# A linear-attention and patch-FFT block pair in one kernel: the normaliser made ahead of its spread, the first contraction behind the inverse transform, and k's first bias from its scaled weight

## The chip, the cores and the metric

The kernel runs on one core of one Trainium2 chip. A time is the time of one execution on the device in microseconds (us); the figure for the kernel before is the median of three runs, 3594.4 us (3587.12 to 3594.8). The profile is of one further execution, which took 3585.28 us.

## What is computed

The input x holds eight images of 384 channels and 64 x 64 pixels, in 32-bit floats. Two blocks follow each other, each with a group norm in front and the input added behind:

```python
def reference(x, ...):
    x = x + attention(_gn(x))       # layer 0
    x = x + patch_filter(_gn(x))    # layer 1
    return x

def _gn(v, G=32, eps=1e-5):         # mean and variance of 12 channels x 64 x 64
    g = v.reshape(B_, G, C_ // G, H_, W_)
    return ((g - mean(g)) / sqrt(var(g) + eps)).reshape(v.shape)

def attention(x):
    q = apply_rope_2d(conv1x1(x, Wq, bq))
    k = apply_rope_2d(conv1x1(x, Wk, bk))
    v = conv1x1(x, Wv, bv)
    q = elu(to_heads(q) * scale) + 1.0            # 6 heads of 64
    k = elu(to_heads(k)) + 1.0
    kv = einsum('bhnd,bhne->bhde', k, v)
    k_sum = k.sum(axis=2)
    normalizer = einsum('bhnd,bhd->bhn', q, k_sum)[..., None]
    out = einsum('bhnd,bhde->bhne', q, kv) / (normalizer + 1e-06)
    return conv1x1(out, Wfc, bfc)

def patch_filter(x):
    t = einsum('bchw,oc->bohw', x, w_in)
    tf = rfft2(patches_of_8x8(t)) * fft_filter
    t = irfft2(tf)
    t = depthwise_conv_3x3(t, w_dw)
    x1, x2 = t[:, :192], t[:, 192:]
    return einsum('bchw,oc->bohw', gelu(x1) * x2, w_out)
```

## The kernel before

**Tiles.** An image is 4096 tokens, cut into eight bands of 512 (8 rows of 64 pixels). The 384 channels lie as three tiles of 128 partitions. A band of x is one tile of 128 x 3 x 512. Every matmul writes a tile of the pool psum, which has eight buffers, all taken in turn under one tag; most larger intermediates share nine buffers of the pool work under the tag "w".

**Stages of an image.** First, while the image before is in its layer 1, its keys: per band and quarter of a band (128 tokens) pk (L421) projects x to k, px (L387) turns the same tokens of x, and later acc (L437) adds k by x into three sums. Instead of normalising x, the kernel scales the weight's rows (scale_weight) and adds a bias (k_bias, q_bias, v_bias). k_bias takes the group sums of wk, which sum_weight (L337) made once at image 0, with a matmul of one row of 32 groups.

Second, the queries of the image (queries, L801). q_project (L510) makes one band: nine matmuls pq in three thirds, on VectorE and ScalarE the bias and the rotation (L531, L545, L546, L547), then elu + 1 in three operations (L333, L334, L335), the last of which, L335 on VectorE, completes the band. q_normalise (L551) needs such a whole band and the sums of k: 12 matmuls pn (24 records in the trace), then on VectorE and ScalarE L564 to L572 make from them 1 / (normaliser + 1e-6), split into three bf16 parts. q_spread (L575) spreads these parts over the channels with 12 matmuls prb and multiplies them into q. project_out (L593) makes pf = mt x q, nine matmuls, and adds it to x (L601); mt is the product of k's sums, wv and wfc, made once per image by kv_finish (L446) in four steps, the last of them pm (L499) with nine copies. The loop runs over the bands: pq of band j + 2, then spread of j, then pn of j + 1, then pf of j - 1. At j = 2 output() contracts the last band of the image before; from j = 2 on the norm chain of the next image's layer 0 is advanced one step at a time (layer0_chain, L744).

Third, the norm of layer 1 (norm_chain, L260): four small groups of matmuls on PE, ps_m, ps_mc, ps_v, ps_r, with small VectorE operations and one square root (L299, with the load of ScalarE's table) between them. The main loop (L899) puts one quarter of the next image's keys behind each of them, then two more quarters, the chain's end, and the rest of the keys of band 1. The group that names a wait on hf is the normalised band, three ScalarE operations (L328), for the first matmuls of layer 1.

Fourth, layer 1 over the bands: pi (w_in), pd (forward transform), tf (times the filter, L635), pb (inverse transform, L644) into one of two ring buffers, the first tap (L691), and one band behind, the other eight taps on VectorE (L705, 24 operations of 512 columns per band), the gate (L711 to L714) and contract (L720): pw with w_out, addition to x (L735), the store of the band. At j = 2 and j = 3 contract(j - 2) stands between the forward and the inverse transform of band j; from j = 4 on behind the keys. Between these steps run the next image's keys, and stream_stats reads x of the image after it for its norm.

**Order.** The kernel is written for the Tile framework, which places the waits; PE's instructions stand in the order of the program, which is what the order of the calls of queries and of the main loop settles. VectorE's and ScalarE's instructions are ordered by the framework's scheduler. Loads and stores are issued from SP. The last image has no keys of a next image and runs its layer 1 in a loop of its own (L955).

Of the kernel before, what the change touches and what calls it, by code (L numbers as in the profile page):

```python
# [14 lines left out]
P = 128  # L15
C = 384
CT = 3
H = W = 64
N = H * W
NBAND = 8  # L20
# [3 lines left out]
NG = 32  # L24
# [92 lines left out]
def conv_blocks_kernel(ctx: ExitStack, tc: tile.TileContext, a: dict, out: bass.AP, nb: int):  # L117
# [142 lines left out]
    def norm_chain(b, layer, params):  # L260
# [52 lines left out]
        if layer == 0:  # L313
            shift = group_tile("shift")
            nc.vector.scalar_tensor_tensor(shift, gm, -1.0, rsg, ALU.mult, ALU.mult)
            params.append(shift)
# [33 lines left out]
    def k_bias(b, params):  # L350

        p_ = ps_tile(f"pbk_{b}")
        nc.tensor.matmul(p_[:, :C], params[2].to_broadcast([NG, P]), group_w["wk"], start=True, stop=True)
        t = small.tile([P, C], F32, tag="kbias", name=f"kbias_{b}", bufs=1)
        nc.vector.tensor_add(t, p_[:, :C], bk_bc)
        return t
# [236 lines left out]
    def project_out(b, j, q, mt):  # L593
        for m in range(CT):
# [6 lines left out]
            nc.vector.scalar_tensor_tensor(xm, p_, bfc[:, m : m + 1], xm, ALU.add, ALU.add)  # L601
        if j == 1:
            differences[b] = taps_pool.tile([P, CT, BT], F32, tag="dw", name=f"differences_{b}")
# [140 lines left out]
    def layer0_chain(b, prepared):  # L744
# [5 lines left out]
        for i, _ in enumerate(norm_chain(b, 0, params)):  # L750
            if b == 0 and i == 3:
                sum_weight(wk, "wk")
            yield
        scale_weight(wk, params)
        yield
        prepared += params, wk, k_bias(b, params)
# [44 lines left out]
    def queries(b, keys, gate, output):  # L801
# [12 lines left out]
        ahead = q_normalise(b, 0, q[0])  # L814
        for j in range(NBAND):
            rn = ahead
            if j < NBAND - 2:
                run(q_project(b, j + 2, wq, qbias, q))
# [5 lines left out]
            q_spread(b, j, q[j], rn)  # L824
            if j == 0:
                gate()
            if j < NBAND - 1:
                ahead = q_normalise(b, j + 1, q[j + 1])
            if j >= 1:
                project_out(b, j - 1, q.pop(j - 1), mt)  # L830
# [8 lines left out]
        project_out(b, NBAND - 1, q.pop(NBAND - 1), mt)  # L839
# [59 lines left out]
    for b in range(nb):  # L899
# [3 lines left out]
        chain, first, second = norm_chain(b, 1, params), keys.project(0), keys.project(1)  # L903
        for _ in range(4):
            next(chain)
            next(first, None)
        for _ in range(2):
            next(second, None)
        run(chain)
        run(second)  # L910
        if b == nb - 1:
            break
        for j in range(NBAND + 1):
            project = keys.project(j - 1 if j > 2 else NBAND)
            fill = chain_of(project, keys.accumulate(j if j < 2 else j - 2 if 3 < j < NBAND else NBAND))
            if j < NBAND:
                tf = []
                layer1 = expand_filter(b, j, normalised(b, j, params, (8, 8), "f"), tf)
# [4 lines left out]
                if j in (2, 3):  # L923
# [6 lines left out]
                first_taps(b, j)  # L930
            else:
# [22 lines left out]
    h = normalised(b, 0, params, (8, 8), "f")  # L954
# [58 lines left out]
```

## Time and profile before

| what | value |
|---|---|
| median of three runs | 3594.4 us (3587.12 to 3594.8) |
| the profiled execution, time on the device | 3585.28 us |
| its span, first to last instruction | 3583.5 us |
| mean clock granted to TensorE | 0.987 |
| VectorE, largest group: L705, the taps | 1055.4 us in 1520 operations |
| TensorE, largest group: L421, pk | 542.2 us in 1536 matmuls |
| ScalarE, largest group: L388, px copied out | 121.9 us in 256 operations |
| one image, start of its queries to start of the next one's | 439.5 us |
| mean traffic of the DMA queues | 81 GB/s |

Engines are named PE (TensorE's matmuls), PEld (its weight loads), DVE (VectorE), ACT (ScalarE), POOL (GpSimd) and SP (the queue that issues loads and stores). In a line of a timeline the first number is the start in us from the span's start, the second the length from the first instruction of the group to the end of its last; then engine, line of the kernel, operation, output <- inputs by the program's names, partitions x elements, and the number of records. A bracket at the end tells how long the engine had been idle and for what. In a table by windows there stand for each window its length, then busy time of the engines PE, PEld, DVE, ACT, POOL with the number of instructions that began there, the clock granted to PE, the share of the DMA engines' time, and GB/s. A list of waits names engine, the waiting operation, and the operation whose end ended the wait, then the sum, the number and the longest.

### The profile page before, as it was taken

The page shows a single profiled execution, that of the slowest core. Times are in us where ns is not written, and L with a number is a line of the kernel's source. Part 1 is how long each engine was busy: PE and PEld are TensorE (multiplying, and loading weights), DVE is VectorE, ACT ScalarE, POOL GpSimd, SP SyncE. Part 2 cuts the span into 40 slices and gives each one's busy share as a digit, 9 for nine tenths or more (in the row PEclk, how much of TensorE's full clock was granted, in tenths as well). Part 3 has the DMA queues.
Part 4 walks back from the last instruction along what each step waited for, and adds up shares of the span by engine and source line. Part 5 has one row for each costly group of instructions (what it writes and reads, how often), then busy time and mean ns, then how long its engine had stood idle before and what let it go on. Part 6 is the DMA issues. An engine that isn't in the chain of part 4 may idle for free.

```text
span 3583.5 us, 38458 instructions
## 1 busy us (share of the span) xinstructions
PE 3450.4 (96%) x14384; PEld 1881.5 (53%) x14384; DVE 2887.9 (81%) x4499; ACT 1810.7 (51%) x3242; POOL 123.0 (3%) x305
## 2 busy tenths in 40 slices
PE   7999999999999999999999999999999999999898
PEld 4544565455554555545564455644555445554454
DVE  6576898868987689885998759987699866997688
ACT  4445563456544565445653455534555354544453
POOL 0000000000000000000000000000000000000011
PEclk9999999999999999999999999999999999999999
DMA  6311223212322122321223212222123211222013
GB/s 212 105 61 50 80 89 120 74 51 71 106 105 75 47 78 99 114 78 45 97 71 126 66 45 97 92 105 66 45 97 113 95 54 36 71 78 80 21 42 91
DMA packets 124608, 290.76 MB, mean 81 GB/s; under 512 B 26069, under 2 KB 36486, under 8 KB 116230
## 3 DMA queue, kind: packets, MB, share of 16 engines
q1 hardware_dynamic: 123078, 282.39, 22.9%
q0 software_dynamic: 1008, 5.51, 0.8%
q8 instruction: 113, 1.85, 0.2%
q14 instruction: 73, 0.60, 0.1%
q10 hardware_dynamic: 336, 0.41, 0.0%
HBM read 232.44 MB, written 50.33 MB: 79 GB/s over the span
## 4 chain that ended last, share of the span: by engine, by line
PE 74%; DVE 20%; ACT 3%; issue 2%; DMA 0%; POOL 0%; SPq 0%; ACTq 0%; POOLq 0%
PE pf L597 13%; PE acc L437 12%; PE pk L421 12%; PE pq L517 12%; DVE dw L705 10%; PE pi L613 8%; PE pw L729 7%; PE pb L644 3%; PE px L387 2%; PE pd L627 2%; PE pn L556 1%; DVE qc L335 1%; DVE x L735 1%; DVE kc L424 1%; ACT ring L651 1%
## 5 line engine op out<-in xcount | busy, mean ns | idle before, releaser
L705 DVE SCALAR_TENSOR_TENSOR dw<-ring,w_dw,dw 128x512 f32<-128x512 f32 x1520 | 1055.4, 746 | 110.4 <-ACT dw L691 90.3
L421 PE MATMUL pk<-wk,x 128*128 128x384 f32 x1536 | 542.2, 490 | 0.1
L597 PE MATMUL pf<-qc,mt 128*128 128x512 f32 x1152 | 527.6, 614 | 0.0
L437 PE MATMUL acc<-xk,kc 128*128 128x385 f32 x1536 | 515.9, 488 | 10.8 <-DVE kc L335 10.8
L613 PE MATMUL pi<-w_in,hf 128*128 128x384 f32 x1536 | 510.2, 489 | 10.3 <-ACT hf L328 10.3
L517 PE MATMUL pq<-x,wq 128*128 128x512 f32 x1152 | 511.6, 596 | 0.7
L437 PEld LDWEIGHTS acc<-xk,kc 128*128 128x128 f32 x1536 | 287.5, 190 | 228.8 <-issue 46.0
L613 PEld LDWEIGHTS pi<-w_in,hf 128*128 128x128 f32 x1536 | 290.7, 191 | 209.9 <-ACT hf L328 12.1
L729 PE MATMUL pw<-gated,w_out 128*128 128x512 f32 x768 | 355.6, 612 | 15.0 <-DVE gated L714 14.5
L421 PEld LDWEIGHTS pk<-wk,x 128*128 128x128 f32 x1536 | 276.0, 190 | 170.4 <-issue 16.5
L597 PEld LDWEIGHTS pf<-qc,mt 128*128 128x128 f32 x1152 | 221.2, 196 | 271.9 <-issue 258.9
L517 PEld LDWEIGHTS pq<-x,wq 128*128 128x128 f32 x1152 | 214.9, 190 | 262.4 <-issue 243.0
L388 ACT COPY xk<-px 128x384 f32<-128x384 f32 x256 | 121.9, 477 | 388.1 <-PE px L387 388.1
L620 ACT COPY ht<-pi 128x384 f32<-128x384 f32 x256 | 121.8, 476 | 249.8 <-PE pi L613 237.4
L601 DVE SCALAR_TENSOR_TENSOR x<-pf,bfc,x 128x512 f32<-128x512 f32 x192 | 142.0, 740 | 125.7 <-PE pf L597 125.7
L729 PEld LDWEIGHTS pw<-gated,w_out 128*128 128x128 f32 x768 | 143.8, 195 | 187.1 <-issue 131.8
L545 ACT ACTIVATE qs<-pq,qbias 64x512 f32<-64x512 f32 x128 | 87.4, 683 | 298.0 <-DVE qc L531 264.3
L424 DVE TENSOR_TENSOR kc<-pk,kbias 128x384 f32<-128x384 f32 x256 | 140.9, 551 | 76.9 <-PE pk L421 75.6
L644 PEld LDWEIGHTS pb<-idft,tf 128*128 128x128 f32 x1536 | 180.6, 193 | 29.7 <-DVE tf L635 18.0
L644 PE MATMUL pb<-idft,tf 128*128 128x128 f32 x1536 | 185.4, 277 | 11.0 <-DVE tf L635 11.0
L651 ACT COPY ring<-pb 128x512 f32<-128x512 f32 x192 | 109.2, 581 | 163.4 <-PE pb L644 162.0
L333 ACT ACTIVATE qs<-qc 128x1536 f32<-128x1536 f32 x64 | 95.0, 1484 | 168.3 <-DVE qc L547 158.3
(149 smaller groups left out, 4006.7 us busy)
## 6 DMA issues: line engine op xcount, KB each, us to landing
tq<-in_tq SPq DMA_DIRECT2D x64, 1024.0 KB, 4.6
x<-in_x SPq DMA_DIRECT2D x64, 768.0 KB, 4.5
tk<-in_tk SPq DMA_DIRECT2D x64, 768.0 KB, 4.2
out_dram<-x SPq DMA_DIRECT2D x63, 768.0 KB, 3.3
xs<-in_x SPq DMA_DIRECT2D x56, 768.0 KB, 4.6
x<-y POOLq DMA_DIRECT2D x7, 768.0 KB, 5.7
wk<-in_wk SPq DMA_DIRECT2D x8, 576.0 KB, 4.0
wv<-in_wv SPq DMA_DIRECT2D x8, 576.0 KB, 6.0
```

The source lines that it names most:

```text
L388: nc.scalar.copy(xk[:, i, :C], px[:, :C])
L421: nc.tensor.matmul(pk[:, :C], tokens(t), wks[:, t, :], start=(t == 0), stop=(t == CT - 1))
L424: nc.vector.tensor_add(kc[:, i, :], pk[:, :C], bias)
L437: nc.tensor.matmul(acc[m][:, : C + 1], kf[:, i, m * P : (m + 1) * P], xk[:, i, :], start=(j == 0 and i == 0), stop=(j == NBAND - 1 and i = ...
L517: nc.tensor.matmul(p_, wqs[:, t, m * P : (m + 1) * P], xt[b, j][:, t, :], start=(t == 0), stop=(t == CT - 1),)
L597: nc.tensor.matmul(p_, mt[:, t, m * P : (m + 1) * P], q[:, t, :], start=(t == 0), stop=(t == CT - 1))
L601: nc.vector.scalar_tensor_tensor(xm, p_, bfc[:, m : m + 1], xm, ALU.add, ALU.add)
L613: nc.tensor.matmul(p_[:, :C], h[:, t, i * P : (i + 1) * P], w_in[:, t, :], start=(t == 0), stop=(t == CT - 1),)
L644: nc.tensor.matmul(patches[:, k // 2, k % 2], tf[:, k, m * P : (m + 1) * P], idft.rearrange("p (u n) -> p u n", u=2), start=True, stop=True,)
L651: nc.scalar.copy(t[:, m, 1:9, 1 : W + 1].rearrange("p r (b c) -> p r b c", c=8), p_.rearrange("p (b r c) -> p r b c", b=8, r=8),)
L705: nc.vector.scalar_tensor_tensor(acc[:, m], src, wd, acc[:, m], ALU.mult, ALU.add)
L729: nc.tensor.matmul(p_, w_out[:, s, m * P : (m + 1) * P], g[:, s, :], start=(s == 0), stop=(s == 1))
```

## The change

Four things are changed.

1. In queries, q_normalise of band j + 1 is called within q_project of band j + 2: behind its first third (behind its second for j = 0). Before, it was called behind the spread of band j. For band 7 (j = 6, where no further q is projected) it is called behind the first third of project_out of band 5, for which project_out becomes a generator that yields behind m = 0.
2. In the norm chain of layer 1 two quarters of the next image's keys, not one, are run behind the first step; after that one quarter behind each of the next three. normalised for band 0 is called straight behind the chain, before the keys that are left, and its tile is kept in ahead; the loop over the bands and the last image's loop take it from there.
3. contract(b, 0), which stood between the forward and the inverse transform of band 2, is called behind the inverse transform and the first tap of band 2, together with load_x(b + 1, 2). contract(b, 1) at j = 3 stays.
4. For image 0 k_bias no longer uses the group sums of wk: three matmuls of minus the mean (by channel) with the already scaled wk give it. The sum of wk by groups, which the images from 1 on use, is made in layer0_chain for image 1.

```diff
@@ -313,7 +313,7 @@
         if layer == 0:
             shift = group_tile("shift")
             nc.vector.scalar_tensor_tensor(shift, gm, -1.0, rsg, ALU.mult, ALU.mult)
-            params.append(shift)
+            params += shift, minus_mean
 
     def normalised(b, j, params, order, name):
 
@@ -347,10 +347,20 @@
         for i in range(CT):
             nc.vector.tensor_scalar(w[:, i, :], w[:, i, :], params[0][:, i : i + 1], factor, ALU.mult, ALU.mult)
 
-    def k_bias(b, params):
+    def k_bias(b, params, wk):
 
         p_ = ps_tile(f"pbk_{b}")
-        nc.tensor.matmul(p_[:, :C], params[2].to_broadcast([NG, P]), group_w["wk"], start=True, stop=True)
+        if "wk" in group_w:
+            nc.tensor.matmul(p_[:, :C], params[2].to_broadcast([NG, P]), group_w["wk"], start=True, stop=True)
+        else:
+            for t in range(CT):
+                nc.tensor.matmul(
+                    p_[:, :C],
+                    params[3][:, t : t + 1].to_broadcast([P, P]),
+                    wk[:, t, :],
+                    start=(t == 0),
+                    stop=(t == CT - 1),
+                )
         t = small.tile([P, C], F32, tag="kbias", name=f"kbias_{b}", bufs=1)
         nc.vector.tensor_add(t, p_[:, :C], bk_bc)
         return t
@@ -599,6 +609,8 @@
                 )
             xm = xt[b, j][:, m, :]
             nc.vector.scalar_tensor_tensor(xm, p_, bfc[:, m : m + 1], xm, ALU.add, ALU.add)
+            if m == 0:
+                yield
         if j == 1:
             differences[b] = taps_pool.tile([P, CT, BT], F32, tag="dw", name=f"differences_{b}")
         band_sums(b, 1, j, xt[b, j], differences.get(b))
@@ -747,13 +759,13 @@
             return
         wk = load_weight(b, "wk", k_runs) if b else first_wk
         params = []
-        for i, _ in enumerate(norm_chain(b, 0, params)):
-            if b == 0 and i == 3:
-                sum_weight(wk, "wk")
+        if b == 1:
+            sum_weight(wk, "wk")
+        for _ in norm_chain(b, 0, params):
             yield
         scale_weight(wk, params)
         yield
-        prepared += params, wk, k_bias(b, params)
+        prepared += params, wk, k_bias(b, params, wk)
 
     def chain_of(*chains):
         for c in chains:
@@ -811,23 +823,29 @@
         next(finish)
         prepared = []
         chain = layer0_chain(b + 1, prepared)
-        ahead = q_normalise(b, 0, q[0])
+        normaliser = {0: q_normalise(b, 0, q[0])}
         for j in range(NBAND):
-            rn = ahead
+
             if j < NBAND - 2:
-                run(q_project(b, j + 2, wq, qbias, q))
+                project = q_project(b, j + 2, wq, qbias, q)
+                for _ in range(2 if j == 0 else 1):
+                    next(project)
+                normaliser[j + 1] = q_normalise(b, j + 1, q[j + 1])
+                run(project)
             if j == 0:
                 run(finish)
                 mt = done[0]
             if 2 <= j < NBAND - 2:
                 next(chain, None)
-            q_spread(b, j, q[j], rn)
+            q_spread(b, j, q[j], normaliser.pop(j))
             if j == 0:
                 gate()
-            if j < NBAND - 1:
-                ahead = q_normalise(b, j + 1, q[j + 1])
             if j >= 1:
-                project_out(b, j - 1, q.pop(j - 1), mt)
+                output_ = project_out(b, j - 1, q.pop(j - 1), mt)
+                if j == NBAND - 2:
+                    next(output_)
+                    normaliser[j + 1] = q_normalise(b, j + 1, q[j + 1])
+                run(output_)
                 if j < NBAND - 2:
                     next(chain, None)
             if j == 2:
@@ -836,7 +854,7 @@
                 load_x(b + 1, j - 4)
             if j == NBAND - 2:
                 run(chain)
-        project_out(b, NBAND - 1, q.pop(NBAND - 1), mt)
+        run(project_out(b, NBAND - 1, q.pop(NBAND - 1), mt))
         return prepared
 
     for j in range(NBAND):
@@ -900,14 +918,14 @@
         prepared = queries(b, keys, gate, output)
         keys = Keys(b + 1, prepared)
         params = []
-        chain, first, second = norm_chain(b, 1, params), keys.project(0), keys.project(1)
-        for _ in range(4):
+        chain, more = norm_chain(b, 1, params), chain_of(keys.project(0), keys.project(1))
+        for quarters in (2, 1, 1, 1):
             next(chain)
-            next(first, None)
-        for _ in range(2):
-            next(second, None)
+            for _ in range(quarters):
+                next(more, None)
         run(chain)
-        run(second)
+        ahead = normalised(b, 0, params, (8, 8), "f")
+        run(more)
         if b == nb - 1:
             break
         for j in range(NBAND + 1):
@@ -915,12 +933,13 @@
             fill = chain_of(project, keys.accumulate(j if j < 2 else j - 2 if 3 < j < NBAND else NBAND))
             if j < NBAND:
                 tf = []
-                layer1 = expand_filter(b, j, normalised(b, j, params, (8, 8), "f"), tf)
+                h = normalised(b, j, params, (8, 8), "f") if j else ahead
+                layer1 = expand_filter(b, j, h, tf)
                 next(layer1)
                 if j != 3:
                     next(fill, None)
                 run(layer1)
-                if j in (2, 3):
+                if j == 3:
                     contract(b, j - 2)
                     load_x(b + 1, j)
                 if j != 3:
@@ -928,6 +947,9 @@
                     next(fill, None)
                 back_transform(b, j, tf[0])
                 first_taps(b, j)
+                if j == 2:
+                    contract(b, j - 2)
+                    load_x(b + 1, j)
             else:
                 run(keys.accumulate(j - 2))
             run(project)
@@ -951,7 +973,7 @@
 
     make_diagonals()
     b = nb - 1
-    h = normalised(b, 0, params, (8, 8), "f")
+    h = ahead
     for j in range(NBAND):
         tf = []
         layer1 = expand_filter(b, j, h, tf)
```

## Prediction

> **What bounds the kernel now.** The page first. TensorE (PE) is busy for 96% of the span, and the chain that ended last runs through PE for 74% of it and through VectorE (DVE) for 20%:
>
> ```profile
> PE 3450.4 (96%) x14384; PEld 1881.5 (53%) x14384; DVE 2887.9 (81%) x4499; ACT 1810.7 (51%) x3242; POOL 123.0 (3%) x305
> ```
>
> A gain must come out of PE's idle time, so next the waits of PE alone (engine, line waited for, releaser: us, times, longest). The two largest:
>
> ```profile
> PE prb L580 <- DVE parts L572: 44.0, 16, 2.8
> PE pw L729 <- DVE gated L714: 14.5, 7, 2.3
> ```
>
> Behind them stand pi on hf (10.3 us, 8 times) and ps_m on mv (9.0, 8 times). Then the timeline of PE for image 3, start of the queries; the other images repeat it:
>
> ```profile
> 1504.35 7.99 PE L517 MATMUL pq<-x,wq 128*128 128x512 f32 x18
> 1512.18 2.10 PE L499 MATMUL pm<-wfc,kvt_bd 128*128 128x384 f32 x6
> 1514.21 0.35 PE L580 MATMUL prb<-parts,expand 32*128 32x128 bf16 x12
> 1514.49 0.86 PE L556 MATMUL pn<-qc,ks_bd 128*32 128x128 f32 x24
> 1515.44 7.99 PE L517 MATMUL pq<-x,wq 128*128 128x512 f32 x18
> 1526.18 0.34 PE L580 MATMUL prb<-parts,expand 32*128 32x128 bf16 x12 [2.75 <-DVE parts L572]
> ```
>
> These are pq of band 2, pm, prb of 0, pn of 1, pq of 3, prb of 1. Matmuls follow each other at 0.43 us (512 columns), so a third of pq is 2.57 us; pn is 0.79 from its start to the next one's; prb 0.3. PE waits 2.9 us for the parts of band 1. The same happens at prb of band 6 (1613.21, idle 2.76), where no pq covers the normaliser. The other bands show no wait. And DVE over the same stretch:
>
> ```profile
> 1510.48 1.75 DVE L335 SCALAR_TENSOR_TENSOR qc<-qc,qs 128x1536 f32<-128x1536 f32 x1
> ...
> 1521.75 1.76 DVE L335 SCALAR_TENSOR_TENSOR qc<-qc,qs 128x1536 f32<-128x1536 f32 x1 [0.41 <-ACT qs L334]
> ```
>
> L335 is the last step of a band of q: band 1 is ready at 1512.2, band 2 at 1523.5. These two times decide this forecast.
>
> [...] This row is the stretch behind image 2's prb of band 1, which waited 2.9 us (0.50 is PE's clock):
>
> ```profile
> 1087.60:1091.00 3.40, 3.40 (x5) 1.34 (x6) 3.34 (x7) 1.37 (x2) 0.00 (x0) 0.50 0.85 308
> ```
>
> From pq of 2 to pq of 4 the images take 30.73 us (3 and 6), 32.1 to 32.4 (five) and 33.6 (the last): a half-clocked stretch costs 1.65, and it follows six of eight such waits, on average 1.4 us an image. I go by the trace: a PE wait of 2.2 us or more costs its length plus some 1.3. [...]
>
> **Part 1, the normaliser, start of the queries.** pn of band j+1 now stands inside pq of j+2: after its second third for j = 0, after its first for the others. No instruction is added; pn's 24 matmuls, four small DVE and two ACT operations move, and no DMA moves. But pn needs the whole of q of j+1.
> - j = 0: the place is 1504.35 + 2 x 2.57 = 1509.5; q of 1 is ready at 1512.2, and DVE's order before it is unchanged. PE waits 2.7 us. Behind it in PE's queue stands all else: the last third of pq 2, pm, prb, pq 3.
> - j = 1: pq of 2 now ends at 1512.25 + 0.8 + 2.6 = 1515.7 instead of 1512.2. In the trace q of 2 follows that end by 11.3 us (L531, two copies L545, L546, L547, L333, L334, L335, with mt's copies and the four L589 between). Band 1's normaliser now stands before that run, I take 11.0. PE has only pm 2.0, prb 0.3 and a third of pq 2.6 = 4.9 before pn of 2: it waits 6.1. Bounds: 5.4 (1523.5 less 1515.44 + 2.57, nothing shifted) and 6.4 (11.3 less 4.9).
> - The wait of 2.9 at prb of 1 goes, its parts being ready. Waits: +2.7 + 6.1 - 2.9 = +5.9. Clock: two waits (1.05, as part of the first is swallowed by the second, and 1.7) for 1.4: +1.3. An image: +7.2.
>
> **Part 1, the other bands.** For j = 2 there are prb, pf 7.9 and a third of pq between the end of pq 3 and pn of 3, 10.8 us against a run of about 10: nothing. For j = 3 pw adds 5.4: nothing. For j = 4 L335 now stands behind the third L601 and two of wk's scalings: 1.0 + 0.3 + 0.7 + 1.75 = 3.7 us behind pf's end against ps_r 0.8 + 2.6: +0.35. For j = 5 pn of 6 comes 5.1 + 8.3 us before prb of 6: its wait goes, 2.9 and 1.4 of clock (21.5 us from pf 4 to pf 6 where image 0 without half clock takes 20.0): -4.3. pn of 7, now behind a third of pf 5, leaves 5.1 us; its run on DVE and ACT comes to that with the L601 and L173 between: 0 to +0.3, I take 0.
>
> **Part 2, norm chain of layer 1.** ps_m, ps_mc, ps_v stand one quarter of k (2.26 us) later, hf ahead of the last two. That takes away ps_m 1.0, ps_v 0.55, pi 1.4. But ps_r keeps its place one quarter behind ps_v, and ACT's order turns: before,
>
> ```profile
> 1649.42 1.28 ACT L299 ACT_TABLE_LOAD   x1
> 1650.71 0.20 ACT L299 ACTIVATE rsg<-var 32x1 f32<-32x1 f32 x1
> ...
> 1656.56 1.48 ACT L333 ACTIVATE ks<-kc 128x1536 f32<-128x1536 f32 x1 [1.64 <-DVE kc L429]
> ```
>
> now L333 stands in front of the load. k's fourth quarter ends 2.2 us earlier than before, so L429 ends about 1654.1, L333 1655.6, load and square root 1657.1, DVE's five small steps 1658.0. PE reaches ps_r at 1654.5: a new wait of 3.5. pi then starts at 1663.3, before at 1663.4: 0. Clock: three short waits never had it, one of 3.5 will: +1.4. Not in image 7, which has no k to interleave.
>
> **Part 3, contraction of band 0.** The wait at pw is that of band 1:
>
> ```profile
> 1729.64 1.12 PE L729 MATMUL pw<-gated,w_out 128*128 128x512 f32 x2
> 1732.79 6.20 PE L729 MATMUL pw<-gated,w_out 128*128 128x512 f32 x10 [2.02 <-DVE gated L714]
> ```
>
> DVE is at work from 1701 to 1733 almost without a gap, so L714 moves only by one tf product put in front: +0.5. The inverse transform of band 2 at 1712.4 now waits for its tf (L635 ends at 1715.5), some 1.7 us, which shortens the later wait to about 1.6. Half clock (6 of 7 now) is less likely: I take -0.5 an image, bounds -1.1 and +0.5. x's store and the load of the next image's band stand one inverse transform (2.7 us) later on SP; that load is used a stage later: 0.
>
> **Part 4, k's first bias, once.** The sum (six matmuls at half clock, 3.7 us) leaves a stretch in which ps_r waited for it: about -2. The bias becomes six matmuls at 0.32 to 0.65 before pk: +2 to +4. The sum comes back in image 0's queries: 6 x 0.32 = +1.9. Together +3, between +1 and +4.
>
> **Sum.** Images 0 to 6: 7.2 - 4.3 + 0.35 + 0 + 1.4 - 0.5 = +4.15, seven times 29. Image 7: +3.2. Start +3. In all +35: the profiled execution of 3585.3 us (span 3583.5) becomes 3620; the median of the runs shown, 3594.4, 9 us above it, becomes 3629.
>
> **Rivals.**
> - The new waits stay without half clock ([...] image 6's pw waited 2.5 us without). Then -2.75 and -1.4 an image, and contraction at -1.1: 7 x (-0.6) + 0.5 + 3 = about 0, 3594. Against it: six of eight waits of 2.9 had it.
> - Faster: q comes in time for pn. Then the waits at both prb, those of part 2 and pw's clock go, 4.3 + 4.3 + 3 + 1 = 12.6 an image, about 3500. It decides from the sum of the two new waits with their clock: below 7.4 us an image instead of 11.5, the change gains. For it: 1.2 us of mt copies lie inside q's run; against: both L335 rows above.
> - Heavier: a wait of 6 us half-clocks two windows, and the first slows q's run: +3 to +4 an image, 3655.
>
> **Chances.** Forecast 0.62, no half clock 0.16, faster 0.10, heavier 0.12. All low ends together give 3583, all high ends 3664; for 8 in 10 I take 3590 to 3656. 0.2% (7 us) is what can be told from no change: faster 0.14 (that rival and the low edge of the second), same 0.13, slower 0.73.
>
> **What would show it.** A row of waits PE pn on DVE qc L335, 16 times, some 70 us; one of ps_r on rsg L306, 7 times, 25 us; prb on parts gone; half clock at the start of every image's queries and before its layer 1. I am wrong if pn waits less than 5 us an image in all, or if ps_r does not wait.

## The result: slower by 1.7%, and the profile after

The changed kernel takes 3651.9 us (median of four runs, 3651.25 to 3653.77) against 3591.5 for the kernel before on the same chip (3587.12 to 3594.8): a ratio of 1.0170, 95% interval 1.0152 to 1.0187, or 60 us more (some 64 against the 3587 that more runs of the kernel before gave on other chips). The forecast was 3629 with a range of 3590 to 3656. Profile against profile, which the sections below use, it is 3650.2 against 3583.5 us: 66.7.

Page of the changed kernel, busy time by engine, then the chain that ended last (the lines behind L347 have moved by 10 to 22: pn is L566, prb L590, pq L527, pf L607, pw L741, pb L656, the products that make tf L647):

```profile
PE 3476.6 (95%) x14388; PEld 1889.1 (52%) x14388; DVE 2916.6 (80%) x4499; ACT 1813.3 (50%) x3242; POOL 120.9 (3%) x305
...
PE 78%; DVE 16%; ACT 3%; issue 1%; POOL 1%; DMA 0%; SPq 0%; ACTq 0%; POOLq 0%
```

PE has only four more records than before, yet 26 us more of busy time: mostly matmuls that ran at half clock. By the profile's records of the granted clock PE is busy for 118.9 us at 0.50, before for 83.6, and half of the difference, 17.7 us, is lost by it; the mean granted clock is 0.979, before 0.987. The other 40 us are waits. PE's waits in the changed kernel (engine, waiting operation, what ended the wait: sum, times, longest):

```profile
PE pn L566 <- DVE qc L335: 66.7, 16, 5.7
PE ps_r L277 <- DVE rsg L306: 27.5, 9, 3.5
PE pb L656 <- DVE tf L647: 22.0, 16, 2.3
...
PE pw L741 <- DVE gated L726: 5.9, 7, 0.9
PE pd L639 <- DVE kc L434: 4.7, 7, 1.4
...
PE pq L527 <- ACT qs L555: 3.1, 8, 0.4
...
PE pi L625 <- ACT hf L328: 1.4, 1, 1.4
```

The rows of before are gone or small: prb on parts (44.0), pw on gated (14.5, now 5.9), pi on hf (10.3). In their place stand pn on qc and ps_r on rsg (1.4 before), and pb on tf has doubled (11.0 before).

Starts of the same matmuls in both profiles give what each stretch of an image costs. Sums over all images, changed minus before, in us:

| stretch | sum | an image |
|---|---|---|
| start of the kernel to the first pq | +2.8 | |
| pq of band 2 to pq of band 4 | +67.3 | +5.8 to +10.3 |
| pq of 4 to pf of 4 | +7.1 | +0.9 |
| pf of 4 to pf of 6 | -32.5 | -4.1 |
| pf of 7 to the first pi (norm of layer 1) | +19.4 | +2.5 (image 0 +4.1, last +0.7) |
| pb of 1 to pb of 4 (part 3) | +3.7 | -0.6 to +0.9 |
| all else | -1.2 | |

**The queries' start.** PE of image 3 (start, length, operation; in brackets the idle time before it):

```profile
1540.64 0.86 PE L566 MATMUL pn<-qc,ks_bd 128*32 128x128 f32 x24 [2.60 <-DVE qc L335]
1541.43 2.84 PE L527 MATMUL pq<-x,wq 128*128 128x512 f32 x6
1544.11 2.10 PE L509 MATMUL pm<-wfc,kvt_bd 128*128 128x384 f32 x6
1546.14 0.35 PE L590 MATMUL prb<-parts,expand 32*128 32x128 bf16 x12
1546.88 2.84 PE L527 MATMUL pq<-x,wq 128*128 128x512 f32 x6 [0.39 <-ACT qs L555]
1555.45 1.50 PE L566 MATMUL pn<-qc,ks_bd 128*32 128x128 f32 x24 [5.73 <-DVE qc L335]
1556.88 7.21 PE L527 MATMUL pq<-x,wq 128*128 128x512 f32 x12
```

pn of 1 waits 2.60 and pn of 2 5.73; behind the second one pn takes 1.50 instead of 0.86 and the two thirds of pq 7.21 instead of 12 x 0.43 = 5.2. Two windows of that stretch (length, then busy time of PE and the other engines, then PE's clock) show half clock, 0.50, beginning while PE still waits:

```profile
1553.70:1557.10 3.40, 1.65 (x25) 1.30 (x26) 2.35 (x3) 0.00 (x0) 0.00 (x0) 0.50 0.00 0
1557.10:1560.50 3.40, 3.40 (x5) 1.33 (x6) 1.86 (x4) 0.59 (x2) 0.00 (x0) 0.50 0.00 0
```

VectorE over the same time:

```profile
1544.32 0.75 DVE L541 SCALAR_TENSOR_TENSOR qc<-pq,qbias,cq 128x512 f32<-128x512 f32 x1
...
1553.54 1.76 DVE L335 SCALAR_TENSOR_TENSOR qc<-qc,qs 128x1536 f32<-128x1536 f32 x1 [0.40 <-ACT qs L334]
```

L335, the last step of q of band 2, ends at 1555.3, which is 11.2 us after that band's last pq (1544.1). PE, with pm, prb and a third of pq in its queue, had nothing more to do from 1549.7 on.

**The norm of layer 1.** Between ps_v and ps_r, and so for the square root, three quarters of keys (pk and px) stood on PE before; one stands there now. The calls 2, 1, 1, 1 come out as 2, 1, 2, 1 quarters, because the call that ends band 0's keys also runs the first quarter of band 1's: ps_r keeps its place behind six quarters, but ps_v stands two quarters later, not one as the prediction has it (the description of the change is off by the same quarter). PE before, then changed, image 3:

```profile
1649.27 0.35 PE L269 MATMUL ps_v<-d,groups 128*32 128x1 f32 x6 [0.39 <-DVE d L294]
1649.55 2.20 PE L421 MATMUL pk<-wk,x 128*128 128x384 f32 x6
...
1651.92 2.10 PE L421 MATMUL pk<-wk,x 128*128 128x384 f32 x6
...
1654.18 2.10 PE L421 MATMUL pk<-wk,x 128*128 128x384 f32 x6
...
1656.54 0.82 PE L277 MATMUL ps_r<-rsg,of_group 32*128 32x1 f32 x6
```

```profile
1683.81 2.10 PE L431 MATMUL pk<-wk,x 128*128 128x384 f32 x6
...
1686.16 0.35 PE L269 MATMUL ps_v<-d,groups 128*32 128x1 f32 x6
1686.44 2.20 PE L431 MATMUL pk<-wk,x 128*128 128x384 f32 x6
...
1692.50 0.80 PE L277 MATMUL ps_r<-rsg,of_group 32*128 32x1 f32 x6 [3.53 <-DVE rsg L306]
1693.22 3.83 PE L431 MATMUL pk<-wk,x 128*128 128x384 f32 x6
```

ScalarE of the changed kernel over the same time:

```profile
1688.45 1.48 ACT L333 ACTIVATE ks<-kc 128x1536 f32<-128x1536 f32 x1 [1.70 <-DVE var L297]
1689.95 1.28 ACT L299 ACT_TABLE_LOAD   x1
1691.24 0.20 ACT L299 ACTIVATE rsg<-var 32x1 f32<-32x1 f32 x1
```

L333 stands in front of the table load, as the forecast had it, ps_r waits 3.53, and the next pk takes 3.83 instead of 2.10.

**The contraction.** PE, bands 2 and 3 of image 3's layer 1:

```profile
1750.19 3.00 PE L656 MATMUL pb<-idft,tf 128*128 128x128 f32 x24 [1.63 <-DVE tf L647]
1753.02 5.32 PE L741 MATMUL pw<-gated,w_out 128*128 128x512 f32 x12
...
1767.46 1.12 PE L741 MATMUL pw<-gated,w_out 128*128 128x512 f32 x2
1769.46 4.56 PE L741 MATMUL pw<-gated,w_out 128*128 128x512 f32 x10 [0.87 <-DVE gated L726]
```

The wait of 2.02 at pw of band 1 is split: 1.63 earlier, at pb of 2, and 0.87 where it was.

### The profile page after: what moved, and what is told of

Its sections match the earlier page's. It is cut to its first block, busy times and chain, and to the rows that moved or that the text cites. A ratio compares the mean times of both kernels' runs of the same rounds, so it can differ in the third digit from the quotient of the medians.

```text
span 3650.2 us, 38517 instructions
## 1 busy us (share of the span) xinstructions
PE 3476.6 (95%) x14388; PEld 1889.1 (52%) x14388; DVE 2916.6 (80%) x4499; ACT 1813.3 (50%) x3242; POOL 120.9 (3%) x305
## 4 chain that ended last, share of the span: by engine, by line
PE 78%; DVE 16%; ACT 3%; issue 1%; POOL 1%; DMA 0%; SPq 0%; ACTq 0%; POOLq 0%
PE pq L527 14%; PE pf L607 14%; PE acc L447 12%; PE pk L431 12%; DVE dw L717 9%; PE pi L625 8%; PE pw L741 6%; PE pb L656 4%; PE px L397 2%; PE pd L639 2%; PE pn L566 2%; ACT ring L663 1%; DVE qc L335 1%; DVE kc L439 1%; DVE kc L434 1%
## 5 line engine op out<-in xcount | busy, mean ns | idle before, releaser
L431 PE MATMUL pk<-wk,x 128*128 128x384 f32 x1536 | 557.7, 501 | 0.0
L527 PE MATMUL pq<-x,wq 128*128 128x512 f32 x1152 | 542.2, 617 | 3.1 <-ACT qs L555 3.1
L607 PE MATMUL pf<-qc,mt 128*128 128x512 f32 x1152 | 511.5, 598 | 0.0
L431 PEld LDWEIGHTS pk<-wk,x 128*128 128x128 f32 x1536 | 283.5, 195 | 179.3 <-issue 30.4
L527 PEld LDWEIGHTS pq<-x,wq 128*128 128x128 f32 x1152 | 217.8, 196 | 263.3 <-issue 250.1
L741 PE MATMUL pw<-gated,w_out 128*128 128x512 f32 x768 | 344.8, 596 | 6.5 <-DVE gated L726 5.9
L607 PEld LDWEIGHTS pf<-qc,mt 128*128 128x128 f32 x1152 | 213.6, 190 | 252.3 <-issue 235.3
L741 PEld LDWEIGHTS pw<-gated,w_out 128*128 128x128 f32 x768 | 140.6, 190 | 167.6 <-issue 134.1
L656 PE MATMUL pb<-idft,tf 128*128 128x128 f32 x1536 | 186.7, 277 | 22.0 <-DVE tf L647 22.0
L656 PEld LDWEIGHTS pb<-idft,tf 128*128 128x128 f32 x1536 | 180.4, 192 | 42.2 <-DVE tf L647 33.9
L555 ACT ACTIVATE qs<-pq,qbias 64x512 f32<-64x512 f32 x128 | 87.4, 683 | 204.0 <-DVE qc L541 194.0
L333 ACT ACTIVATE qs<-qc 128x1536 f32<-128x1536 f32 x64 | 95.0, 1484 | 171.9 <-DVE qc L557 161.8
```

The costliest lines, as they stand in the source:

```text
L431: nc.tensor.matmul(pk[:, :C], tokens(t), wks[:, t, :], start=(t == 0), stop=(t == CT - 1))
L527: nc.tensor.matmul(p_, wqs[:, t, m * P : (m + 1) * P], xt[b, j][:, t, :], start=(t == 0), stop=(t == CT - 1),)
L607: nc.tensor.matmul(p_, mt[:, t, m * P : (m + 1) * P], q[:, t, :], start=(t == 0), stop=(t == CT - 1))
L656: nc.tensor.matmul(patches[:, k // 2, k % 2], tf[:, k, m * P : (m + 1) * P], idft.rearrange("p (u n) -> p u n", u=2), start=True, stop=True,)
L741: nc.tensor.matmul(p_, w_out[:, s, m * P : (m + 1) * P], g[:, s, :], start=(s == 0), stop=(s == 1))
```

## The experiments

Each kernel ran four or more times beside the kernel before; times are medians, ratios are to the kernel before on the same chip (3586.5 to 3587.8 us). The changed kernel's 3651.9 was measured beside 3591.5, so a difference to it carries some 4 us. Diffs are cut, with ... for what is left out.

**u1: the three other parts without the normaliser's.** The body of queries is that of the kernel before (its diff is to the changed kernel).

```diff
-                normaliser[j + 1] = q_normalise(b, j + 1, q[j + 1])
-                run(project)
...
+            if j < NBAND - 1:
+                ahead = q_normalise(b, j + 1, q[j + 1])
```

> The changed kernel with the normaliser's part undone (pn stands behind the spread again, for all bands); the other three parts stay. Additive theory: by sections of an image the part costs 67.3 us from pq of 2 to pq of 4, 7.1 from there to pf of 4, and saves 32.5 from pf of 4 to pf of 6, in all 41.9 over eight images; without it 3652 - 42 = 3610 us, within 5. PE's wait at prb for parts comes back with 16 x 2.8 = 44 us, pn's wait for qc (66.7) is gone, ps_r's wait (27.5) and the sections of layer 1 stay within 0.3 us an image. Rival: the later stages lost time only because the first one came late (half clock, full buffers); then ps_r's wait or the sections from the norm to band 4 shrink too, and the time is 3600 or less.

3617.8 us (ratio 1.0085, 1.0070 to 1.0100). Waits as the additive theory has them: prb 44.0, no pn, ps_r 27.1. But the norm section costs 3.5 us an image over before instead of 2.5, and the time is 8 us above the expectation. The same wait is followed by more half clock. PE of u1, image 3:

```profile
1677.98 1.40 PE L277 MATMUL ps_r<-rsg,of_group 32*128 32x1 f32 x6 [3.46 <-DVE rsg L306]
1679.31 4.21 PE L431 MATMUL pk<-wk,x 128*128 128x384 f32 x6
```

Here ps_r itself takes 1.40 and pk 4.21, twice the 2.10 that six pk take at full clock; in the changed kernel 0.80 and 3.83, after a wait that is 0.07 longer.

**o1: the kernel before with the normaliser's part alone** (the same diff the other way round).

> The kernel before with the normaliser's part alone. Additive theory: 3591.5 + 42 = 3634 us, within 5; PE waits 67 us at pn for qc in 16 waits, prb does not wait, the norm section keeps its three short waits (ps_m, ps_v, pi) and no ps_r row. Rival: the parts disturb each other; then this run is above 3642 or below 3626, and with the run without the part the two don't add up to the whole of 60.

3634.4 us (1.0129, 1.0112 to 1.0146). That it hits the expected 3634 to the microsecond is luck: against the 3587.8 measured beside it the part costs 46.5, not the expected 42. The waits are as expected: pn 66.9 us in 16 waits, prb none, no new one at ps_r. With the 29.9 of the other three alone that makes 76 together, where the whole change costs 60 to 64; so in this the rival was right: the parts do not add up. The sections say where the excess lies: in the norm stretch (24.9 in u1, 19.4 in the changed kernel) and, in o1, at pb of 2 to pb of 4, which o1 doesn't touch (between -0.9 and +2.2 an image). pw waits 2.0 to 2.3 there as before; but half clock follows it in two images only (before in six of seven). In the other five PE comes to pd of band 4 earlier and waits there 1.0 instead of 0.2, and in three of these half clock follows that wait.

**late12: pn of bands 1 and 2 alone back behind the spread.**

```diff
-                normaliser[j + 1] = q_normalise(b, j + 1, q[j + 1])
+                if j not in (0, 1):
+                    normaliser[j + 1] = q_normalise(b, j + 1, q[j + 1])
                 run(project)
...
+            if j in (0, 1):
+                normaliser[j + 1] = q_normalise(b, j + 1, q[j + 1])
             if j >= 1:
```

> The changed kernel with pn of bands 1 and 2 alone back behind the spread; pn of 3 to 7 stays ahead. If the price is q's readiness at j = 0 and 1: pq of 2 to pq of 4 returns to the 32 us of before (prb of 1 waits 2.9 again), pf of 4 to pf of 6 stays at 17.4, and the time is 3652 - 67 = 3585 us, within 5: slightly below the kernel before. Rival: moving pn at all reorders VectorE, so the wait only moves on to prb of 2 or pn of 3; then the gain is under 45 us, and a new PE row of over 15 us shows.

3594.6 us (1.0015, 1.0007 to 1.0024). The rival falls: no PE row of over 15 us is new, prb waits 8 times for 22.1 in all, pq of 2 to 4 is within 1.6 us of before (image 0, which now makes a sum of wk there, +3.7), and pf of 4 to 6 is 17.4. 57 of the expected 67 us came; of the rest 6 are the norm section again, 3.5 an image here against 2.5. So two of the seven moved pn cost nearly all of it (63 us between the two profiles in pq of 2 to 4); the later ones bring the 32.5 and cost the 7.1 of pq of 4 to pf of 4.

**thirds3: pn of bands 1 and 2 behind all three thirds.**

```diff
-            if m < CT - 1:
+            if m < CT - 1 or j >= 2:
                 yield
...
-                for _ in range(2 if j == 0 else 1):
+                for _ in range(3 if j < 2 else 1):
                     next(project)
```

> The changed kernel with pn of bands 1 and 2 behind all three thirds of the next pq (instead of two and one). If the price is only how long PE must wait for q (ready 2.77 and 5.89 us after PE gets to pn now, and a third of pq takes 2.57): the waits fall to about 0.2 and 0.75 us, no half clock follows, and pq of 2 to pq of 4 falls from 40.5 to about 32; eight images give 8 x 8.5 = 68, the time 3584 us, within 6. Rival: q is not ready at a fixed time, but a fixed run after PE's pq and behind the normaliser's own steps on VectorE; then pn of 2 still waits 2 us or more, with half clock, and the gain is 45 or less.

3584.0 us (0.9989, 0.9982 to 0.9995). The same normaliser, moved by 2.6 and 5.1 us in PE's queue, is 68 us faster, and the rival falls. pq of 2 to 4 falls to 29.2 (image 0: 31.3), below the 30.7 to 33.6 of before, and no half clock follows there. That the sum is the expected 68 is luck, though: between the two profiles this stretch gives back 88.7 us, pq of 4 to pf of 4 loses 17.2 and the norm 4.6. The wait has not gone without a trace:

```profile
PE pn L566 <- DVE qc L335: 13.4, 7, 1.9
...
PE pf L607 <- DVE qs L541: 4.4, 8, 0.6
```

pn of 3, behind a third of pq of 4, now waits 1.9 in seven of the eight images, and in two of them half clock follows.

**c0back: the contraction of band 0 back between the transforms.**

```diff
-                if j == 3:
+                if j in (2, 3):
                     contract(b, j - 2)
                     load_x(b + 1, j)
...
-                if j == 2:
-                    contract(b, j - 2)
-                    load_x(b + 1, j)
```

> The changed kernel with the contraction of band 0 back between the transforms of band 2. The waits of that part, told from the sections: pb of 2 waits 2.1 for tf and pw of 1 waits 1.0 in the changed kernel, against 2.2 at pw alone before. If these are the part's whole price, and half clock falls where it will, the three sections from pb of 1 to pb of 4 change by +0.75 an image without a half-clocked window and by -0.9 with one fewer: the time is 3652 within 8, and PE's row pw on gated is back at 14.4 us, that of pb on tf at 11. Rival: the part costs more elsewhere (x's store and load come later); then the sections outside pb of 1 to pb of 4 shrink as well, and the time falls below 3640.

3653.0 us (1.0179, 1.0162 to 1.0196), the changed kernel's 3651.9 within what can be told apart: part 3 is worth nothing that shows, either way. The rows are back at 14.4 and 11 (pb on tf 10.9).

**psv: ps_v one quarter of k earlier.**

```diff
-        chain, more = norm_chain(b, 1, params), chain_of(keys.project(0), keys.project(1))
-        for quarters in (2, 1, 1, 1):
+        chain, first, second = norm_chain(b, 1, params), keys.project(0), keys.project(1)
+        for quarters in (2, 1, 1):
             next(chain)
             for _ in range(quarters):
-                next(more, None)
+                next(first, None)
+        next(chain)
+        for _ in range(2):
+            next(second, None)
+        more = second
```

> The changed kernel with ps_v one quarter of k earlier (quarters 0, 1 / ps_m / 2 / ps_mc / 3 / ps_v / 4, 5 / ps_r / hf / 6, 7): two quarters instead of one cover the square root. If ps_r's wait is made by the one quarter left in front of it and by L333 ahead of the table load: ps_r's wait goes from 27.5 to under 4 us, its half clock with it, ps_v waits some 0.55 a time; the norm section falls from 33.9 by about 5 us in each of seven images, 3652 - 35 = 3617 us. Rival: what follows is bound by ScalarE; the wait moves to pi for hf (1 to 1.5 us each, 7 times) and the gain is 25 or less.

3634.0 us (1.0132): 18 of the expected 35, and the rival's place was wrong too, since pi does not wait. Of 19.2 us between the two profiles only 9.0 lie in the norm; 4.6 lie in pq of 2 to 4 and 6.3 in pb of 1 to 4, where PE waits as long as in the changed kernel and less of the time is at half clock (mean granted clock of the whole profile 0.982 against 0.979). ScalarE loads its table right behind ps_v now, but ps_r still waits 2.5 in each of seven images. VectorE of psv, from the square root on:

```profile
1680.87 0.14 DVE L300 RECIPROCAL rsg<-rsg 32x1 f32<-32x1 f32 x1
...
1681.56 1.75 DVE L439 TENSOR_TENSOR kc<-kc,ks 128x1536 f32<-128x1536 f32 x1
1683.22 0.14 DVE L303 TENSOR_TENSOR y<-rsg 32x1 f32<-32x1 f32 x1
...
1683.82 0.14 DVE L304 TENSOR_TENSOR y<-y,var 32x1 f32<-32x1 f32 x1
1683.94 0.96 DVE L414 TENSOR_TENSOR ks<-kc,tk 128x768 f32<-128x768 f32 x1
1684.82 0.13 DVE L305 TENSOR_SCALAR y<-y 32x1 f32<-32x1 f32 x1
1684.94 0.96 DVE L422 TENSOR_TENSOR kc<-kc,tk 128x768 f32<-128x768 f32 x1
1685.81 0.14 DVE L306 TENSOR_TENSOR rsg<-rsg,y 32x1 f32<-32x1 f32 x1
```

Five steps of 0.14 take 5.1 us, because the keys' operations stand between them in VectorE's order. In the changed kernel the same five follow each other in 0.9 us (1691.48 to 1692.36), since the keys' work is already done while the square root is late.

**ahead: the quarters of k as before, hf still straight behind the chain.**

```diff
-        chain, more = norm_chain(b, 1, params), chain_of(keys.project(0), keys.project(1))
-        for quarters in (2, 1, 1, 1):
+        chain, first, second = norm_chain(b, 1, params), keys.project(0), keys.project(1)
+        for _ in range(4):
             next(chain)
-            for _ in range(quarters):
-                next(more, None)
+            next(first, None)
+        for _ in range(2):
+            next(second, None)
+        more = second
```

> The changed kernel with the quarters of k as before (one behind each step of the norm chain), but hf of band 0 still called straight behind the chain. If the new wait of ps_r comes from the quarters alone: it is gone (1.4 us in all are left), ps_m 1.0 and ps_v 0.55 are back, pi does not wait for hf (before 1.4 an image); the norm section is 30.1 us, against 33.9 now and 31.5 before, so 7 x 3.8 = 27, the time 3625 us. Rival: hf ahead on ScalarE and VectorE delays the keys' own work, and PE waits at pk or acc for it; then the section stays at 31 or more, and the time at 3632 or more.

3626.5 us (1.0105), as expected. ps_r's row is down to 2.8, and the norm section is 30.1 us: the call of normalised ahead of the last quarters is a gain of 1.35 an image on its own; the quarters (2, 1, 1, 1) turned it into a loss.

**best1 and best2: putting the places together, on the kernel before.** best1, without the two generators' yields and the call for hf, which is that of the changed kernel:

```diff
+                project = q_project(b, j + 2, wq, qbias, q)
+                if j in (0, 5):
+                    for _ in range(1 if j else 3):
+                        next(project)
+                    ahead = q_normalise(b, j + 1, q[j + 1])
+                run(project)
...
-            if j < NBAND - 1:
+            if j in (2, 3, 4, 6):
                 ahead = q_normalise(b, j + 1, q[j + 1])
...
+                if j == 1:
+                    next(output_)
+                    ahead = q_normalise(b, j + 1, q[j + 1])
...
-                if j in (2, 3):
+                if j == 2:
                     contract(b, j - 2)
...
-            if j > 3:
+            if j > 2:
                 contract(b, j - 2)
```

> The kernel before with pn of 1 behind all of pq of 2, pn of 2 behind the first third of pf of 0, pn of 6 behind the first third of pq of 7, hf of band 0 straight behind the norm chain, and contract(b, 1) behind the keys of its stage, as from band 2 on. If the waits of before are what the sections say: both prb waits of 2.9 with their half clock go (8 x 8.3 = 66, less 0.4 an image for pn between the thirds), pi's wait goes (7 x 1.4 = 10), pw's wait goes (7 x 2.2, with half clock in most: 20): 3590 - 93 = 3497 us. Rival: VectorE is the next bound at the queries' start and at band 3, and the waits come back at prb of 1 or 2 and at pb or pd of band 4; then 3550 or more.

3543.5 us (0.9875, 0.9860 to 0.9889): 44 gained, half of what was expected and near the rival's 3550. Two places were wrong:

```profile
PE pb L646 <- DVE tf L637: 35.6, 16, 3.7
PE pn L556 <- DVE qc L335: 18.6, 8, 2.3
```

pb of band 3, without the contraction in front of it, waits 3.7 for tf: VectorE sets the pace there, as the rival had it, though one band earlier (1.6 us lost between pb of 1 and the image's end, where 20 were to be gained). And pn of 7, left behind the spread of 6, which no longer waits, comes 2.3 us before its q (pf of 4 to 6 gains 8.3 us, in best2 32.5).

best2 leaves the contraction as in the kernel before and takes pn of 5, 6 and 7 from the change:

```diff
-                if j in (0, 5):
+                if j in (0, 4, 5):
...
-            if j in (2, 3, 4, 6):
+            if j in (2, 3):
                 ahead = q_normalise(b, j + 1, q[j + 1])
...
-                if j == 1:
+                if j in (1, 6):
                     next(output_)
                     ahead = q_normalise(b, j + 1, q[j + 1])
```

> The kernel before with pn of 1 behind all of pq of 2, pn of 2 and of 7 behind the first third of pf of 0 and of 5, pn of 5 and 6 behind the first third of pq of 6 and 7, pn of 3 and 4 as before, and hf of band 0 straight behind the norm chain; the contraction as before. From the sections of earlier runs, an image: pq of 2 to 4 -3.3 (best1), pf of 4 to 6 -4.1 (the changed kernel), pn between thirds +0.5, norm -1.4 (best1, seven images): 8 x -6.9 - 9.8 = -65, so 3587 - 65 = 3522 us, within 6. Rival: with pn of 4 late as before and pn of 5 early, the normaliser's run of 5 waits behind that of 4, q of 6 is late as in best1, and the wait of 2.3 at pn of 6 stays: 3540 or more.

3522.7 us (0.9820, 0.9803 to 0.9836), as expected; neither prb nor pn is left in PE's list of waits.

**best3 and best4: the quarters.** best3 puts one quarter of keys in front of the contraction of band 1:

```diff
                 run(layer1)
+                if j == 3:
+                    next(fill, None)
                 if j in (2, 3):
                     contract(b, j - 2)
```

> As best2, and at band 3 one quarter of the keys of band 2 (2.26 us of PE) ahead of contract(b, 1). If VectorE's end of the gate is fixed there: the quarter fills the wait of 2.2 at pw, which also took half clock in most images, and the stretch from pb of 1 to pb of 4 falls by 2.2 to 3.9 an image: 7 x 3.2 = 22 us below best2, some 3500 us. Rival: VectorE is the bound in this stretch and kc's addition (0.55) or the keys' products stand in front of the gate; then pw waits as long as before behind the quarter, and the gain is 8 us or less.

3517.4 us (0.9808, 0.9794 to 0.9823): 5 better than best2, so the rival's side. pw's row is gone, but px of the quarter waits 1.5 for VectorE's tf, and pi of band 4 waits 0.65 for hf. The stretch from pb of 1 to pb of 4 falls by 2.5 to 2.8 us in six images (in the seventh it grows by 3.1), and 1.4 of that comes back behind it: two matmuls of acc have only moved there (0.65), and pd of band 6 takes 0.74 longer. The start of the kernel, which the edit does not touch, was 4.6 us longer in this profile than in best2's.

best4 is best3 with the quarters of the norm set so that three cover the square root:

```diff
-        for _ in range(4):
+        for quarters in (2, 1, 1):
             next(chain)
-            next(first, None)
-        for _ in range(2):
+            for _ in range(quarters):
+                next(first, None)
+        next(chain)
+        for _ in range(3):
             next(second, None)
```

> As best3, with the quarters of k in the norm of layer 1 set 2, 1, 1, then three between ps_v and ps_r, and one behind hf. In psv the five small steps behind the square root ended on VectorE 5 us behind its start, between the keys' work, 2.5 us too late for ps_r with two quarters in between; with three it should be in time. Then ps_m's wait of 1.0 is gone, ps_r does not wait, and pi waits for hf by 2.8 (rs, three hf operations) less one quarter of 2.26 = 0.6: the section falls from 30.1 to about 29.7, 3 us in all, near what can be told. Rival: VectorE's chain slips again behind the additional quarter, ps_r or pi waits 2 us or more, and the kernel is slower than best3 by 10 or more.

3507.7 us (0.9780, 0.9766 to 0.9795): the fastest, 2.2% ahead of the kernel before and 3.9% ahead of the changed one, and 9.7 ahead of best3 where 3 were expected. Between these two profiles 7.9 us are the norm section, which is 28.9 us instead of the expected 29.7 (before 31.5, changed 33.9); another 3.6 are the start of the kernel, which the edit does not touch. Of the norm's four groups only ps_r waits, 0.1 us; pi waits 0.2 in the first image alone, and the last image has waits of its own. Mean clock 0.995 against 0.987 before and 0.979 changed; the page's PE line:

```profile
PE 3430.7 (98%) x14384; PEld 1865.5 (53%) x14384; DVE 2890.0 (82%) x4499; ACT 1806.7 (52%) x3242; POOL 129.3 (4%) x305
```

## Why the prediction came true, point by point

**Right in sign, place and mechanism.** pn waits for qc 16 times for 66.7 us ("16 times, some 70"), ps_r for rsg seven times for 3.5 ("7 times, 25"; the list's 27.5 holds the first norm and the last image as well, 1.5 and 1.4), prb's row is gone, and the start's two waits of 2.60 and 5.73 were put at 2.7 and 6.1. late12 and thirds3 show that the cause is q's readiness at j = 0 and 1: later places in the same queue give back 57 and 68 us, in pq of 2 to 4 alone 63 and 89. The gain at prb of 6, -4.3 in the sum, is -4.1. The run of q of 2 behind its pq, taken as 11.0, is 11.2.

**Too small by half: 35 forecast, 60 to 67 measured.** The terms of the sum, over all images, between the two profiles:

| term | forecast | measured | what it was |
|---|---|---|---|
| start of the queries, waits and clock | +58 | +67 | clock, a switch, image 0's sum of wk |
| pq of 4 to pf of 4 | +3 (L335 at j = 4) | +7 | pn of 5 doesn't wait; a switch at four pn |
| prb of 6 | -34 | -32.5 | image 0 had no half clock to lose |
| norm of layer 1 | +10 | +19 | the wait as long, but 0.8 later; more clock |
| contraction | -3.5 | +3.7 | waits added, no clock gained that holds |
| start of the kernel, k's first bias | +3 | +2.8 | and 2.1 in the first row |

- *Clock.* The forecast took 1.3 us an image for two waits at the start of the queries. With waits of 5.7 net of the one removed, 0.4 for the pn switches, 0.2 for a new wait of pq (its buffer is read late by L555) and 0.3 for image 0's sum of wk, 1.8 of the 8.4 us are left for it. The granted clock tells where: behind the second wait it is at half for 6.83 us in all eight images (in image 3 from 1553.69 on), twice the 3.41 us that the shortest half-clocked stretches last; behind the first wait for 3.41 us in three of them, and for 6.83 in image 5 (+10.3). The rival "heavier" thus had the two windows right. Its price of 3 to 4 more an image was wrong, since a part of the 6.83 us falls into the wait itself (1.76 us in image 3) and q's run was not stretched (11.2 us). That the time, 3652, is nearer to its 3655 than to the forecast is luck: most of what is missing lies in other stretches.
- *The switch.* In the changed kernel the first pq behind a pn starts 0.2 us behind the start of the last of pn's records (image 3: 1541.43 after 24 records of pn from 1540.64), and the sections tell the price: from pq of 4 to pf of 4, where PE neither waits nor runs at half clock, one pn between thirds of pq adds 0.2 us an image (best1), two add 0.4 (best2), the four of the changed kernel 0.9. "No instruction is added" was right, and yet the new places cost something that the forecast put at nothing.
- *The norm.* The wait has the length of the forecast (3.5), but all of it lies later. PE arrives at ps_r 23.4 us behind the first pf of band 7, where the working had 22.6: it took 2.0 off the 24.7 of the kernel before, whose waits on this way are only 1.2 (0.83 at ps_m, 0.39 at ps_v). VectorE and ScalarE come later too, so the wait ends 26.9 behind that pf instead of 26.1; with a clock loss of 1.7 that is +2.5 an image. Other runs with the same wait lost 21 to 26 us in this section.
- *The contraction.* pb's wait (1.7 forecast, 1.6 measured) came; pw's fell to 0.9 where 1.6 was expected. But pd then waits for kc (4.7 us in seven waits, before 1.9), and a half-clocked stretch follows the group of short waits behind it in five images. VectorE, with no gap of over 0.25 us from 1738 to 1800, set the end of the stretch. The +3.7 is not a settled price: with the same instructions and the same waits the stretch came out between -2.6 (psv) and +5.4 (ahead), which is put down to half clock as an estimate, and with the contraction back (c0back) it is still +2.3.
- *The bias.* From ps_v to the first pk 8.1 us, before 5.7: +2.4. In image 0's queries the sum of wk adds 2.1 (thirds3: 31.3 us from pq of 2 to 4 in image 0, 29.2 in the others). This was read from sections of single profiles, and the start of the kernel moves by a microsecond or more between profiles without an edit there; no run had the part alone.

**Why a wait has no fixed price.** The profile records the granted clock; in the kernel before half clock comes in 23 stretches, in the changed one in 28. In each of these two profiles all of them but the last (2.78 and 3.09 us, at the end of the trace) last 3.41 us or two to five times as long, up to 17.07, and begin on one grid with that period, to within 0.01 us. Waits of one length were not followed by half clock of one length: of the sixteen waits of 2.75 us at prb in the kernel before, thirteen were followed by half clock, three not. The price of a wait differed likewise from place to place: ps_r's wait of 3.5 cost 2.5 us an image over before in one kernel and 3.5 in another, and in thirds3 2.4 to 4.1 from image to image. A price per wait ("length plus some 1.3") is an average at best. The parts, measured alone, exceed the whole by 12 to 16 us; in the sections the excess lies where half clock fell differently, in the norm (u1) and at pb of 2 to pb of 4 (o1). No run shows that this is all of it.

## What to carry to other kernels

An operation that needs the last result of another engine's run is placed by that run's end: take the end from the trace (here L335), lay it against the queue of the waiting engine, and move the consumer until work of the same length stands in front of it; 2.6 and 5.1 us of matmuls made 68 us of difference. Small steps between two matmuls (a square root, five products) need cover not by their own 0.14 us each but by what the scheduler puts between them (psv: 5.1 us from the first of five to the last, in the changed kernel 0.9). And where half clock had followed the waits that were removed, the gain was larger than the waits: best4 took PE's idle share from 4% to 2% and the mean clock from 0.987 to 0.995; of the 77.6 us between the two profiles 57.9 are idle time and 19.7 busy time of PE.

## Not expected of the hardware

- Equal waits cost different clock. After 3.46 us idle in u1 and 3.53 in the changed kernel, the following six pk took 4.21 and 3.83 us (2.10 at full clock), the ps_r in front 1.40 and 0.80.
- How much idle time stood before half clock, counted in the profiles of the kernel before and the changed one (without the first 50 and the last 130 us of each), cut into stretches of 3.41 us on that grid: 45 stretches at full clock were followed by a half-clocked one, and in each of them PE ran no matmul for at least 42% of the time; of the 1906 that were followed by another at full clock none was without a matmul for more than 59%. What decides between these two shares stays open. The waits of 2.75 us at prb are shorter than such a stretch; each of the three that half clock did not follow was spread over two stretches, neither of which was idle for more than 49%.
- Where nothing waits, a change of place still cost time: the four pn between pq of 4 and pf of 4 0.9 us an image in the changed kernel, without a wait of 0.1 us or a half-clocked stretch there; see the switch above.
- The same instructions at the start of best3 and best4, without a wait between them: the first 24 records of pk took 10.94 us in the one profile and 7.98 in the other; that half clock alone makes the difference is an estimate, from the ps_r in front, which took 1.44 and 0.82, and from the same 24 records at full clock in the kernel before, 7.98. The start of the kernel carries some 4 us that no edit explains.
